# Router logits with the router's weights stationary, and transposed back

## The chip, the cores and the metric

The kernel runs on one core of one Trainium2 chip. The metric is the device time of one execution in microseconds (us); the numbers below are the median of six executions, and one further execution was profiled. All data are 32-bit floats (some indices are 32-bit integers).

## What is computed

Two layers work on 128 graphs of 64 nodes with 256 features, that is 8192 rows (tokens). Each layer is a graph attention inside every graph, followed by a mixture of 8 experts of which each token uses two. Cut to its core:

```python
# layer 0
x = x + gnn(layernorm(x), adj, W, a)          # attention within 64 nodes, elu
x = x + moe(layernorm(x), router_w, w1, b1, w2, b2)
# layer 1
x = x + gnn(layernorm(x), adj, W, a)          # with a leaky slope of 0.2
x = x + moe(layernorm(x), Wg, bg, bias, W1, b1, W2, b2)

def moe(tokens):                               # tokens: (8192, 256)
    logits = tokens @ router_w.T               # (8192, 8): the router
    top2 of the logits, weights by softmax over the two
    for each expert e:                         # hidden 256 (layer 0), 512 (layer 1)
        h = gelu(tokens @ w1[e] + b1[e])       # relu in layer 1
        y = h @ w2[e] + b2[e]
        out += combine[:, e] * y
```

The part in question is the line `logits = tokens @ router_w.T`: for each token 8 sums over 256 features.

## The kernel before

The 8192 rows are taken in blocks of 512 (`TB`), four tiles (`TT`) of 128 partitions (`P`); 16 blocks per layer, 32 in all, numbered by t in the main loop. Three strands of work are interleaved by hand, in an order that the program writes out: on TensorE, VectorE, ScalarE and SyncE, instructions run in the order in which the Python code issues them.

- `attend` (called `a`) is the attention of one block. It is a Python generator: every `yield` ends a stage, and each call `a(n)` issues one more stage. Stages that matter here: the transposes of the normalized block (line 249, tile `pt_g`), the product with the attention's weights (line 288, tile `pw_g`, copied out by ScalarE at line 295), a small VectorE product (line 299, `sm_g`), the scores (lines 307 and 308, `pe_g`), their maximum on VectorE (line 323) and exponential on ScalarE (line 326), the transposes of the attention (line 337, `pp_g`), copied by VectorE and ScalarE (lines 339 and 340), and the product with them (line 346, `po_g`).
- `route` (called `r`) is the router of one block, a generator too: statistics; normalization into `tn` (line 238); transposes of `tn` (line 249, tile `pt_r`), copied to SBUF as `xt_r`, one half by VectorE (line 253) and one by ScalarE (line 255); the router's product into `pl_r` (line 417) and its copy into `lg` (line 426, or 428 and 429 in layer 1), the choice of the best expert; the second best; an exponential; the places in the experts' lists (lines 474 to 492); the writes of the rows to those lists in DRAM by eight indirect DMAs (line 497, on GpSimd's queue); and `plan` (lines 533 to 600), some twenty small VectorE instructions that decide which expert the next slots of 256 rows belong to.
- `Slots` runs the experts on such slots: `x` transposes 256 rows (line 680, copied at line 684), `h` makes the hidden layer (line 749, activation at line 757, which waits for the biases too), `y` the output (line 777, added to its bias at line 785), which indirect DMAs scatter. In layer 1 the output rows are first weighted (line 817). `fetch` lets SyncE load the rows of coming slots (line 609) after it has read the plan's table (line 604), and `ahead` loads the experts' weights.

In the router's product the token tile is the stationary operand (128x128, loaded for every matmul) and the router's weights, 8 columns, are the moving one. The output has tokens on partitions and experts along the free dimension. A 32-bit matmul shows up as two weight loads and two matmul instructions in the profile, a 32-bit transpose as one of each.

The PSUM pool `ps_c` has two buffers for tag "a" (attention) and two for tag "r" (router); the SBUF tag "ex" has three buffers.

Turn t of the main loop (lines 933 to 982) issues stages of the attention of block t+1, of the routing of block t, the last stage of the routing of block t-1 (`r(t - 1)`, the plan), the first two of block t+1 (`r(n)`), and calls of `h`, `x`, `y`. Around the change the order is:

```python
        h(); x(); a(n)       # a(n): the product of line 288
        r(t - 1)             # the plan
        a(n)                 # line 299
        h()
        r(t)                 # transposes of line 249
        slots.fetch()
        if more: x()
        a(n)                 # lines 307 to 326
        r(t)                 # the router's product, lg, first choice
```

Blocks 0 to 2 are worked through before the loop by the list `chains`, in which each turn pops one stage from each chain.

Of the kernel before, what the change touches and what calls it, by code (L numbers as in the profile page):

```python
# [8 lines left out]
F32 = mybir.dt.float32  # L9
# [7 lines left out]
P = 128  # L17
NG = 64
D = 256
KD = D // P  # L20
E = 8
TT = 4
TB = TT * P
# [12 lines left out]
def adj_ffn_kernel(  # L36
# [33 lines left out]
    nc = tc.nc  # L70
# [18 lines left out]
    work = ctx.enter_context(tc.tile_pool(name="work", bufs=3))  # L89
    small = ctx.enter_context(tc.tile_pool(name="small", bufs=2))  # L90
    slot = ctx.enter_context(tc.tile_pool(name="slot", bufs=2))
    ps_c = ctx.enter_context(tc.tile_pool(name="ps_c", bufs=2, space=bass.MemoryType.PSUM))
# [25 lines left out]
    ident = const.tile([P, P], F32, name="ident")  # L118
# [5 lines left out]
    for g in range(2):  # L124
        r = slice(g * NG, (g + 1) * NG)
# [10 lines left out]
    start = const.tile([P, E], F32, name="start")  # L136
# [48 lines left out]
    rw = [const.tile([P, KD, E], F32, name=f"rw{l}") for l in range(2)]  # L185
# [57 lines left out]
    def transposed(src, tag, ptag, name, both):  # L243

        xt = work.tile([P, KD, TB], F32, tag=tag, name=f"xt_{name}", bufs=2)
        for k in range(KD):
            pt = ps_c.tile([P, TB], F32, tag=ptag, name=f"pt_{name}_{k}")
            for t in range(TT):
                nc.tensor.transpose(
                    pt[:, t * P : (t + 1) * P], src[:, t, k * P : (k + 1) * P], ident  # L250
                )
            if k % 2 == 0 and not both:
                nc.vector.tensor_copy(xt[:, k, :], pt)  # L253
            else:
                nc.scalar.copy(xt[:, k, :], pt)
        return xt
# [143 lines left out]
    def route(l, b, blk):  # L400

        name = f"r{l}_{b}"
# [8 lines left out]
        yield  # L411
        tT = transposed(tn, "tT", "r", name, l == 0 and b < FIRST)
        yield
        pl = ps_c.tile([P, TT, E], F32, tag="r", name=f"pl_{name}")
        for t in range(TT):
            for k in range(KD):
                nc.tensor.matmul(  # L417
                    pl[:, t, :],
                    lhsT=tT[:, k, t * P : (t + 1) * P],
                    rhs=rw[l][:, k, :],  # L420
                    start=(k == 0),
                    stop=(k == KD - 1),
                )
        lg = small.tile([P, TT, E], F32, tag="lg", name=f"lg_{name}")
        if l == 0:
            nc.vector.tensor_copy(lg, pl)
# [27 lines left out]
        r = slice(b * TT, (b + 1) * TT)  # L454
# [161 lines left out]
    class Slots:  # L616
# [117 lines left out]
        def h(self):  # L734
            k = self.nh
            self.weighted()
            if k == self.nx or k == self.ny + 2:
                return
            self.nh += 1
            sl = self.all[k]  # L740
            l = sl["l"]
            wc, xT = sl["wc"], sl["xT"]
            hT = slot.tile([P, HC[l], SL], F32, tag="hT", name=f"hT_s{k}")
            for f in range(0, HC[l], 2):
                ph = ps_s.tile([P, 2, SL], F32, tag="ph", name=f"ph_s{k}_{f}", bufs=2)
                for j in range(2):
                    for c in range(KD):
                        o = c * HC[l] * P + (f + j) * P
                        nc.tensor.matmul(  # L749
                            ph[:, j, :],  # L750
                            lhsT=wc[:, o : o + P],
                            rhs=xT[:, c, :],
                            start=(c == 0),
                            stop=(c == KD - 1),
                        )
                for j in range(2):
                    nc.scalar.activation(  # L757
                        hT[:, f + j, :], ph[:, j, :], AF.Gelu if l == 0 else AF.Relu,
                        bias=wc[:, OB1[l] + f + j : OB1[l] + f + j + 1],
                    )  # L760
            sl["hT"] = hT
            if l == 1 and sl["rest"]:
                self.spare(k)

        def y(self):
            k = self.ny
            self.weighted()
            if k == self.nh:
                return
            self.ny += 1  # L770
            sl = self.all[k]
            l = sl["l"]
            wc, hT = sl["wc"], sl["hT"]
            py = ps_s.tile([P, ST, D], F32, tag="py", name=f"py_s{k}")
            for t in range(ST):
                for f in range(HC[l]):
                    nc.tensor.matmul(  # L777
                        py[:, t, :],
                        lhsT=hT[:, f, t * P : (t + 1) * P],
                        rhs=wc[:, O2[l] + f * D : O2[l] + (f + 1) * D],  # L780
                        start=(f == 0),
                        stop=(f == HC[l] - 1),
                    )
            ys = slot.tile([P, ST, D], F32, tag="ys", name=f"ys_s{k}", bufs=4)
            nc.vector.tensor_tensor(  # L785
                ys, py, wc[:, OB2[l] : OB1[l]].unsqueeze(1).to_broadcast([P, ST, D]), ALU.add
            )
            sl["ys"] = ys
            for t in range(ST):
                if l == 0:  # L790
                    ins = nc.gpsimd.indirect_dma_start(  # L791
                        out=res[sl["part"]],
                        out_offset=self.row(sl, t),
                        in_=ys[:, t, :],
                        in_offset=None,
                        bounds_check=2 * N - 1,
                        oob_is_err=False,
                    )
                    unordered(f"res{sl['part']}", ins)
            if l == 1:  # L800
                self.ready = k
            self.ahead()
# [57 lines left out]
    def there(i):  # L860
        return 0 <= i < len(blks) and blks[i]

    def load(i, first=None):
        if there(i):
            k = blks[i]
            if k["l"]:
                assert all(s["l"] or s["part"] != part(k["b"]) for s in slots.all[slots.ny :])
            k["in"] = load_block(k["l"], k["b"], first)
            k["a"] = attend(k["l"], k["b"], k)

    def a(i, n=1):
        if there(i):
            for _ in range(n):
                next(blks[i]["a"], None)

    def r(i, n=1):
        if there(i):
            k = blks[i]
            if "r" not in k:
                k["r"] = route(k["l"], k["b"], k)  # L880
            for _ in range(n):
                next(k["r"], None)
# [15 lines left out]
    place = counted("place", [P, ST], [[P, ST]], 0, 1)  # L898
    att = lambda b: [(a, b)] * 9 + [(a, b, 2), (a, b)]
    chains = [  # L900
        (0, att(0)[3:] + [(r, 0)] * 10),
        (1, att(1)[2:] + [(r, 1)] * 10),
        (2, att(2) + [(r, 2)] * 9),
        (8, att(3) + [(r, 3)] * 2),
        (12, [(a, 4)] * 3),
    ]
# [26 lines left out]
    for t in range(FIRST, len(blks)):  # L933
        n = t + 1
        more = slots.nf - slots.ny > SB or len(slots.all) - slots.ny > SB
        if t + 3 != NB:
            load(t + 3)
        a(n)
        h()
        x()  # L940
        a(n)
        r(t - 1)
        a(n)
        h()
        r(t)
        slots.fetch()
        if more:
            x()
        a(n)
        r(t)  # L950
        if t + 2 != NB:
            a(t + 2)
        y()
        a(n)
        (h if more else x)()
        r(t)
        a(n)
        y()
        a(t + 2, 1 + (t + 2 == NB))
        if more:  # L960
            x()
        a(n)
        r(t)
        h()
        a(n)
        if more:
            y()
        x()
        a(n)
        h()  # L970
        r(n)
        y()
        a(t + 2)
        r(t)
        r(t)
        y()
        slots.fetch()
        x()
        r(n)
        r(t)  # L980
        if t + 3 == NB:
            load(t + 3)
# [57 lines left out]
```

## Time and profile before

| | |
|---|---|
| median of 6 executions | 1726.02 us (1723.2 to 1731.31) |
| profiled execution, its own time | 1729.69 us |
| its span in the profile | 1727.8 us |
| mean granted TensorE clock | 0.888 |
| instructions | 22826 |

How to read the profile: PE is TensorE's matmuls, PEld its weight loads (they overlap PE), DVE is VectorE, ACT ScalarE, POOL GpSimd, SP SyncE; a "q" behind a name is that engine's sequencer or queue. A line of a group or of the order in time names the line of the code, the engine, the operation, the tile written and after the arrow the tiles read, the shape, and how many. In the list of costly groups the numbers behind the bar are busy time in us, mean duration of one in ns, then the engine's idle time just before them and what ended most of it. In the order of time the first two numbers are start and length in us, and in brackets stands the idle time before and what ended it; "remote" there means that the wait ended by an event which fits no end of an instruction at that time. In the list of waits the numbers are the sum in us, how often, and the longest. In the table by stretches, PEclk is the granted TensorE clock as a share of the full one. Each instruction of a row with "x16" is pipelined with the next, so the time to the next row's start says more than the length.

Some more entries of the profile that the prediction uses:

| group | count | mean ns |
|---|---|---|
| line 417, weight load 128x128 for `pl_r` | 512 | 241 (median 192 of a quiet turn) |
| line 249, transposes `pt_r` | 256 | 288 |
| line 255, ScalarE copy 128x512 | 35 | 586 |
| line 253, VectorE copy 128x512 of `pt_r` | 29 | 691 |
| line 340, ScalarE copy 64x256 | 32 | 364 |
| line 295, ScalarE copy 128x258 | 128 | 375 |

### The profile page before, as it was taken

To read this page: it belongs to the slowest core of one execution; us is meant where nothing else is said; L and a number is where in the kernel's file an instruction comes from. 1 tells how busy PE (TensorE), PEld (TensorE's weight loads), DVE (VectorE), ACT (ScalarE), POOL (GpSimd) and SP (SyncE) were. 2 spreads that over 40 slices of the span, in tenths; PEclk is the share of its full clock that TensorE was granted. 3 is DMA by queue.
4 is the path that set the end of the run, shared out by engine and by line. 5 is a ranking of instruction groups with operands and counts; after the bars stand their busy time and mean duration, and the time that the engine had idled before them with its cause. 6 is when DMAs were issued, how large, how long until landed. Compare 5 with 4: busy or idle time off the path is not lost. (4 is left out here: it accounts for less than half of the span.)

```text
span 1727.8 us, 22826 instructions
## 1 busy us (share of the span) xinstructions
PE 1352.0 (78%) x6436; PEld 1141.9 (66%) x6436; DVE 883.0 (51%) x3404; ACT 669.5 (39%) x1567; POOL 766.5 (44%) x742
## 2 busy tenths in 40 slices
PE   6657776767777667666668798888889888889997
PEld 4546655655556546555557677777778777778896
DVE  4555755564454555745555554555556554332332
ACT  4534444444444434333334333333343333223332
POOL 3254544444444454334444355345454444544333
PEclk9668988888888889878889889999999898999999
DMA  6545555575554665656565577577786656688774
GB/s 188 138 144 182 171 159 166 165 213 161 159 177 140 213 201 161 218 165 187 187 208 164 155 224 236 160 202 210 200 229 198 171 142 185 170 232 245 201 205 70
DMA packets 267198, 315.42 MB, mean 183 GB/s; under 512 B 41399, under 2 KB 224318, under 8 KB 267072
## 3 DMA queue, kind: packets, MB, share of 16 engines
q1 hardware_dynamic: 222240, 227.80, 43.5%
q0 software_dynamic: 44832, 86.17, 18.8%
q8 instruction: 51, 0.84, 0.2%
q14 instruction: 75, 0.61, 0.1%
HBM read 215.03 MB, written 102.51 MB: 184 GB/s over the span
## 5 line engine op out<-in xcount | busy, mean ns | idle before, releaser
L749 PE MATMUL ph_s<-xT_s,wc_s 128*128 128x256 f32 x1760 | 430.4, 396 | 64.0 <-DVE xT_s L684 27.9
L777 PE MATMUL py_s<-wc_s,hT_s 128*128 128x256 f32 x1760 | 442.9, 405 | 14.3 <-issue 14.0
L749 PEld LDWEIGHTS ph_s<-xT_s,wc_s 128*128 128x128 f32 x1760 | 343.8, 199 | 132.4 <-DVE xT_s L684 36.4
L777 PEld LDWEIGHTS py_s<-wc_s,hT_s 128*128 128x128 f32 x1760 | 350.3, 204 | 66.6 <-issue 16.6
L820 POOL DMA_INDIRECT out_dram<-ys_s,to_s x142 | 222.9, 1570 | 348.4 <-ACT ys_s L817 244.9
L757 ACT ACTIVATE hT_s<-ph_s,wc_s 128x256 f32<-128x256 f32 x440 | 183.2, 470 | 305.8 <-issue 132.7
L497 POOL DMA_INDIRECT lists<-tn_r,ix_r x256 | 248.7, 972 | 107.5 <-issue 72.4
L791 POOL DMA_INDIRECT res<-ys_s,to_s x156 | 160.1, 1026 | 293.3 <-DVE erc_g L332 179.5
L288 PE MATMUL pw_g<-gw,xt_g 128*128 128x258 f32 x512 | 156.6, 460 | 163.8 <-ACT wh_g L295 134.6
L288 PEld LDWEIGHTS pw_g<-gw,xt_g 128*128 128x128 f32 x512 | 111.1, 229 | 196.2 <-ACT wh_g L295 141.2
L684 DVE COPY xT_s<-px_s 128x512 f32<-128x512 f32 x149 | 102.2, 686 | 234.2 <-remote 151.0
L785 DVE TENSOR_TENSOR ys_s<-py_s,wc_s 128x512 f32<-128x512 f32 x149 | 103.0, 691 | 212.1 <-PE py_s L777 198.9
L817 ACT ACTIVATE ys_s<-ys_s,cf_s 128x256 f32<-128x256 f32 x142 | 64.1, 499 | 148.5 <-DVE ys_s L785 148.3
L417 PE MATMUL pl_r<-rw,xt_r 128*128 128x8 f32 x512 | 81.0, 292 | 47.5 <-DVE xt_r L253 38.5
L417 PEld LDWEIGHTS pl_r<-rw,xt_r 128*128 128x128 f32 x512 | 80.7, 241 | 54.7 <-DVE xt_r L253 42.8
L295 ACT COPY wh_g<-pw_g 128x258 f32<-128x258 f32 x128 | 46.4, 375 | 177.7 <-remote 85.5
L238 ACT ACTIVATE tn_r<-xb_g,nb_r,rs_r 128x256 f32<-128x256 f32 x128 | 66.4, 589 | 81.4 <-DVE nb_r L236 39.2
L238 ACT ACTIVATE xn_g<-xs,nb_g,rs_g 128x256 f32<-128x256 f32 x128 | 66.4, 589 | 64.5 <-DVE nb_g L236 64.5
L680 PE MATMUL px_s<-ident,xg_s 128*128 128x128 f32 x596 | 91.3, 276 | 0.0
L680 PEld LDWEIGHTS px_s<-ident,xg_s 128*128 128x128 f32 x596 | 75.4, 145 | 12.5 <-issue 0.6
L277 POOL TENSOR_SCALAR cap_g<-adj 128x256 f32<-128x256 int32 x32 | 34.6, 1082 | 93.8 <-DMA adj<-in_adj_dram 64.2
L346 PE MATMUL po_g<-wh_g,pT_bd 128*128 128x256 f32 x256 | 69.3, 418 | 7.7 <-ACT pT_bd L340 5.6
(474 smaller groups left out, 1569.7 us busy)
## 6 DMA issues: line engine op xcount, KB each, us to landing
wc_s<-in_w_dram SPq DMA_DIRECT2D x142, 512.0 KB
wc_s<-in_w_dram SPq DMA_DIRECT2D x156, 256.0 KB
xg_s<-lists SPq DMA_DIRECT2D x78, 258.0 KB
xg_s<-lists SPq DMA_DIRECT2D x71, 260.0 KB
yb<-res SPq DMA_DIRECT2D x16, 1024.0 KB
wc_s<-bcat SPq DMA_DIRECT2D x78, 129.0 KB
wc_s<-bcat SPq DMA_DIRECT2D x71, 130.0 KB
xs<-in_x_dram SPq DMA_DIRECT2D x16, 512.0 KB
```

The lines of the kernel that those rows point to most:

```text
L238: nc.scalar.activation(outs(t), xb[:, t, :], AF.Identity, bias=nb[:, t : t + 1], scale=rs[:, t : t + 1])
L288: nc.tensor.matmul(pw, lhsT=xt[:, k, t * P : (t + 1) * P], rhs=gw[l][:, k, :], start=(k == 0), stop=(k == KD - 1),)
L417: nc.tensor.matmul(pl[:, t, :], lhsT=tT[:, k, t * P : (t + 1) * P], rhs=rw[l][:, k, :], start=(k == 0), stop=(k == KD - 1),)
L497: ins = nc.gpsimd.indirect_dma_start(out=lists[l], out_offset=bass.IndirectOffsetOnAxis(ap=ix[:, k, t : t + 1], axis=0), in_=tn[:, t, 0 : ...
L680: nc.tensor.transpose(px[:, c, t * P : (t + 1) * P], xg[:, t, c * P : (c + 1) * P], ident)
L684: nc.vector.tensor_copy(xT, px)
L749: nc.tensor.matmul(ph[:, j, :], lhsT=wc[:, o : o + P], rhs=xT[:, c, :], start=(c == 0), stop=(c == KD - 1),)
L757: nc.scalar.activation(hT[:, f + j, :], ph[:, j, :], AF.Gelu if l == 0 else AF.Relu, bias=wc[:, OB1[l] + f + j : OB1[l] + f + j + 1],)
L777: nc.tensor.matmul(py[:, t, :], lhsT=hT[:, f, t * P : (t + 1) * P], rhs=wc[:, O2[l] + f * D : O2[l] + (f + 1) * D], start=(f == 0), stop=( ...
L785: nc.vector.tensor_tensor(ys, py, wc[:, OB2[l] : OB1[l]].unsqueeze(1).to_broadcast([P, ST, D]), ALU.add)
L791: ins = nc.gpsimd.indirect_dma_start(out=res[sl["part"]], out_offset=self.row(sl, t), in_=ys[:, t, :], in_offset=None, bounds_check=2 * N - 1,
L820: ins = nc.gpsimd.indirect_dma_start(out=out, out_offset=self.row(sl, t), in_=ys[:, t, :], in_offset=None, compute_op=ALU.add,)
```

## The change

The routing gets one more stage. After the transposes, the router's weights (128x8 for each half of the features) become the stationary operand and the transposed tokens (512 columns) the moving one. The product `pq` has 8 partitions (experts) and 512 columns (tokens). ScalarE copies it to SBUF (`lT`), the stage ends, and in the next stage four transposes bring it back into `pl`, 128 partitions by 8 for each of the four tiles. From `lg` on nothing changes.

`pq` takes a turn in the two PSUM buffers of tag "r", `lT` one in the three SBUF buffers of tag "ex".

As there is one stage more, the order gets one more call: `r(t)` in the main loop ahead of `r(t - 1)`, and one more entry in the chains of blocks 0 to 2. In the loop, the routing transposes are thus issued where the plan stood, then come the plan, `a(n)` and `h()`, then `pq` and its copy where the transposes stood, and the transposes back where the router's product stood.

```diff
         tT = transposed(tn, "tT", "r", name, l == 0 and b < FIRST)
         yield
+
+        pq = ps_c.tile([E, TB], F32, tag="r", name=f"pq_{name}")
+        for k in range(KD):
+            nc.tensor.matmul(
+                pq, lhsT=rw[l][:, k, :], rhs=tT[:, k, :], start=(k == 0), stop=(k == KD - 1)
+            )
+        lT = work.tile([E, TB], F32, tag="ex", name=f"lT_{name}")
+        nc.scalar.copy(lT, pq)
+        yield
         pl = ps_c.tile([P, TT, E], F32, tag="r", name=f"pl_{name}")
         for t in range(TT):
-            for k in range(KD):
-                nc.tensor.matmul(
-                    pl[:, t, :],
-                    lhsT=tT[:, k, t * P : (t + 1) * P],
-                    rhs=rw[l][:, k, :],
-                    start=(k == 0),
-                    stop=(k == KD - 1),
-                )
+            nc.tensor.transpose(pl[:, t, :], lT[:, t * P : (t + 1) * P], ident[0:E, 0:E])
         lg = small.tile([P, TT, E], F32, tag="lg", name=f"lg_{name}")
...
-        (0, att(0)[3:] + [(r, 0)] * 10),
-        (1, att(1)[2:] + [(r, 1)] * 10),
-        (2, att(2) + [(r, 2)] * 9),
+        (0, att(0)[3:] + [(r, 0)] * 11),
+        (1, att(1)[2:] + [(r, 1)] * 11),
+        (2, att(2) + [(r, 2)] * 10),
...
         x()
         a(n)
+        r(t)
         r(t - 1)
         a(n)
         h()
```

## The prediction

> **What bounds the kernel now.** I read the engines' busy shares and the costliest groups first, then the busy time by stretch, then TensorE's waits, then two turns of the main loop in order of time. The page first:
>
> ```profile
> PE 1352.0 (78%) x6436; PEld 1141.9 (66%) x6436; DVE 883.0 (51%) x3404; ACT 669.5 (39%) x1567; POOL 766.5 (44%) x742
> L417 PE MATMUL pl_r<-rw,xt_r 128*128 128x8 f32 x512 | 81.0, 292 | 47.5 <-DVE xt_r L253 38.5
> ```
>
> TensorE is the busiest engine, and the router's product (line 417) has 512 instructions, two for each of 8 matmuls in 32 blocks, with 47.5 us of idle time ahead of them. The stretches (turns t=3 to 20, turns 21 to 31, tail):
>
> ```profile
> core 0: us, PE busy (x) PEld busy (x) DVE busy (x) ACT busy (x) POOL busy (x), PEclk, DMA share, GB/s
> 108.00:957.00 849.00, 598.38 (x2852) 495.10 (x2852) 463.54 (x1761) 347.05 (x754) 381.54 (x383) 0.86 0.57 180
> 957.00:1496.00 539.00, 472.16 (x2239) 406.29 (x2239) 291.33 (x1138) 204.97 (x529) 252.54 (x203) 0.92 0.68 191
> 1496.00:1728.00 232.00, 212.26 (x1070) 187.44 (x1070) 71.85 (x272) 66.68 (x155) 91.40 (x62) 0.96 0.72 187
> ```
>
> TensorE is busy 70%, then 88%, then 91%. What it waits for in the first two stretches:
>
> ```profile
> PE pw_g L288 <- ACT wh_g L295: 126.4, 13, 10.0
> ...
> PE pl_r L417 <- DVE xt_r L253: 38.2, 10, 5.1
> ```
>
> In the first stretch one wait of about 10 us in a turn stands ahead of the attention's product (line 288), before the edit's place; the edit doesn't touch it. In the second the wait stands right at the router's product: 38.2 us in 10 turns. A turn of each kind:
>
> ```profile
> 595.57 3.06 PE L749 MATMUL ph_s<-xT_s,wc_s 128*128 128x256 f32 x8
> 598.46 1.04 PE L249 MATMUL pt_r<-ident,tn_r 128*128 128x128 f32 x8
> 599.34 0.60 PE L680 MATMUL px_s<-ident,xg_s 128*128 128x128 f32 x4
> 599.77 0.60 PE L307 MATMUL pe_g<-sm_g,same 128*128 128x256 f32 x2
> 600.21 0.59 PE L308 MATMUL pe_g<-wh_g,ident 128*128 128x256 f32 x2
> 600.64 1.85 PE L417 MATMUL pl_r<-rw,xt_r 128*128 128x8 f32 x16
> ```
>
> ```profile
> 590.08 0.16 DVE L541 SCALAR_TENSOR_TENSOR lf_p<-du_p,at_r 128x8 f32<-128x8 f32 x1
> 593.47 0.17 DVE L594 TENSOR_TENSOR du_p<-du_p,tk_p 128x8 f32<-128x8 f32 x1
> 596.22 0.42 DVE L299 TENSOR_TENSOR sm_g<-imod,wh_g 128x256 f32<-128x256 f32 x1 [2.59 <-ACT wh_g L295]
> 599.10 0.69 DVE L253 COPY xt_r<-pt_r 128x512 f32<-128x512 f32 x1 [2.46 <-PE pt_r L249]
> 602.52 0.19 DVE L426 COPY lg_r<-pl_r 128x32 f32<-128x32 f32 x1 [0.81 <-PE pl_r L417]
> ```
>
> TensorE runs without a gap here; VectorE does the plan (lines 541 to 594, 3.56 us from 590.08 to 593.64) while it would wait anyway. And in the second stretch:
>
> ```profile
> 1235.74 1.04 PE L249 MATMUL pt_r<-ident,tn_r 128*128 128x128 f32 x8
> 1240.59 0.69 DVE L253 COPY xt_r<-pt_r 128x512 f32<-128x512 f32 x1 [6.57 <-remote]
> 1241.33 0.39 PE L417 MATMUL pl_r<-rw,xt_r 128*128 128x8 f32 x2 [3.69 <-DVE xt_r L253]
> 1241.90 2.14 PE L417 MATMUL pl_r<-rw,xt_r 128*128 128x8 f32 x14 [0.17 <-ACT xt_r L255]
> 1250.57 0.69 DVE L785 TENSOR_TENSOR ys_s<-py_s,wc_s 128x512 f32<-128x512 f32 x1 [1.30 <-PE py_s L777]
> ```
>
> TensorE's transposes are recorded as over at 1236.8, yet VectorE's copy of them starts at 1240.59: their end is seen late. I can't name the cause; it comes back in every turn of this stretch.
>
> **TensorE's own sum, per block.** Removed: 16 instructions of line 417. Their next instruction starts 1.70 us after the first (600.64 to 602.34), 106 ns each. Added: 4 instructions of 512 columns. A 256-column one of line 749 takes 3.45/16 = 216 ns in the chain of waits; by columns 431 ns, so 4 x 431 = 1.73 us. From below, if width cost nothing, 4 x 216 = 0.86. I take 1.73, since the 128-column transposes (0.43 for 4, 109 ns) already show time going with columns. Then 4 transposes with 8 moving columns: at most the 0.43 of four 128-column ones (line 680); at least 0.22, since a transpose's weight load is recorded 51 ns shorter than a product's (139 against 190 ns) and 106 - 51 = 55 ns. I take 0.33. Net 1.73 + 0.33 - 1.70 = +0.36 us, ends -0.62 and +0.46. So the edit doesn't save TensorE time; it splits one product into two dependent pieces with ScalarE between.
>
> [...]
>
> **The added copy.** ScalarE moves 8x512 from PSUM: line 255's 128x512 copy takes 586 ns, and 64 partitions cost no less than 128 (364 against 375 ns), so 0.59; lower end the 128x2 copy's 0.16. Behind it on ScalarE stands the attention's exponential, which waits for later TensorE work; the weighted-output and hidden-layer activations come before it. The added PSUM tile (tag "r", two buffers) and SBUF tile (tag "ex", three) take buffers whose last readers are data it needs anyway or are long done: nothing, and 0.6 us a turn (one copy) if not.
>
> **What moves.** The extra r(t) puts the routing transposes ahead of the plan and of h(). No DMA is issued by that step. On TensorE 0.88 us goes ahead of 2.89 us; on VectorE the copy of line 253 now stands ahead of the plan's 3.56 us and waits for its transposes. SP waits for the plan: its list loads come some 6 us later, at 600.5 instead of 595.0; its next issue waits until 605.17 now, so this hides; without that cover it costs what it passes 605.
>
> First kind of turn, from 595.57: transposes to 596.45, ph 599.34, product 601.07, px 601.50, pe 602.37, transposes back 602.70, against 602.34. VectorE: copy 596.05 to 596.74, plan to 600.30, line 299 to 600.72, 0.78 us before pe needs it. Then the maximum of line 323 ends at 603.33 instead of 601.72, because pe is now behind the product. ScalarE's exponentials (1.34), residual (2.06), table load (1.28), hidden layer (0.84) and half copy (0.36) follow from 603.4 and end at 609.3 instead of 608.63: the product of line 346 moves by +0.66. That I take for 12 turns: 7.9 us. In the last 6 turns of the stretch the attention's transposes (line 337) already wait for VectorE (19.0 us in 7 waits), so they get VectorE's delay, 0.8 at line 426 and 1.6 at line 323; I take 1.3: 7.8. Together +16, ends -11 (18 x -0.62) and +29 (18 x 1.6).
>
> Second kind: the product fills 1.73 us of the wait. If its end is seen at 1240.5 as the present late ends are, ScalarE does the hidden layer to 1241.37, the copy to 1241.96, and the transposes back end near 1242.5 instead of 1243.89: -1.4. The chain behind has slack on VectorE of 0.59 (before line 428) and 1.30 (line 785), so no more than -1.9 can be gained. The copy of line 253 may be seen late, which takes part away; I take -1.0, ten times: -10, ends -19 and +23 (third case below).
>
> The granted clock: it is 0.51 from 1243 to 1250 and 1.00 before and after. A shorter wait may keep it up, but TensorE would then wait for VectorE's chain, so the -1.9 holds still.
>
> [...] In this trace gaps of 2.94 us were followed by half clock in some turns (763 us) and not in others (814.8).
>
> Before the loop three blocks pass through at 51, 71 and 88 us, with gaps around them; copy and transposes add 0.59 + 0.43 each if serial, 3 us, or nothing. I take +2.
>
> Sum: 16 - 10 + 2 = +8 us on the profiled execution's 1729.69 (span 1727.8 and 1.9 around it), 1737.7. That execution lies 3.7 above the median of 1726.02, so for the median: 1734.
>
> **The rivals.** *The second stretch wins.* The wait of 38.2 us speaks for it, VectorE's slack limits it: -19 there, and the first stretch pays only TensorE's +0.36 x 18 = 6.5: 1726 - 12.5 = 1713. *Nothing measurable.* Gain and loss cancel: 1726. *The plan gets stuck.* In the second stretch the transposes' end is seen late by 3.5 us or more in its new place too. The copy at 1240.6 would then hold the plan (to 1244.8), line 299 (1245.3), pe (1246.2), and through VectorE's 3.75 us of line 265 line 337 by +2.3: ten times +23, so 16 + 23 + 2 = +41, 1767. It decides from a copy start later than about 1237. Against it: ScalarE's copies of line 295 are seen on time up to 1232.5, and the transposes would end at 1232.7 and 1233.2. That the edit doesn't do what it says I count to the first rival: a product of 0.86 would take 0.87 off each of 32 blocks, 28 us, at most 1706.
>
> **How the numbers follow.** Forecast 0.49 (1724 to 1746, mostly above 1729.5), first rival 0.27, nothing measurable 0.12, stuck plan 0.12. About 0.2%, 3.5 us, is what a measurement can tell from none. Faster 0.27, same 0.13 (with a little of the forecast), slower 0.60. The range leaves out the far ends of both rivals: 1710 to 1758; the forecast's own is 1724 to 1746.
>
> **What would show it.** Right: four 512-column instructions 430 ns apart; line 253's VectorE copy before line 541 in every turn; line 323 later by about 1.6 us after the long wait in the first stretch; a wait of 2 to 3 us before the transposes back in the second. Wrong: a product nearer 0.9 us, a long wait of the first stretch that changes from 10 us, or line 253 starting after 1237 in a turn of the second (the same place counted from its line 288).

## The result, and the profile after

The changed kernel takes 1731.79 us (median of 23 executions) against 1724.83 us for the kernel before (49 executions on the same chip). The ratio is 1.0036, with a 95% interval from 1.0025 to 1.0048: slower by 7 us. The profiled execution has a span of 1735.7 us against 1727.8. From the product on, line numbers are 2 to 4 higher than before; after the routing they are 2 higher.

The page of the changed kernel, and its groups kept apart by shape (busy time in us, mean ns of one, then the idle time ahead of them and what ended it):

```profile
PE 1351.2 (78%) x6180; PEld 1076.7 (62%) x6180; DVE 878.1 (51%) x3404; ACT 686.6 (40%) x1599; POOL 766.9 (44%) x742
```

```profile
L417 PE MATMUL pq_r<-xt_r,rw 128*8 128x512 f32 x128 | 65.2, 630 | 9.3 <-ACT xt_r L255 5.0 <-DVE xt_r L253 4.3
...
L421 ACT COPY lT_r<-pq_r 8x512 f32<-8x512 f32 x32 | 18.2, 569 | 23.9 <-PE pq_r L417 23.9
L425 PE MATMUL pl_r<-ident,lT_r 8*128 8x8 f32 x128 | 14.6, 219 | 27.9 <-ACT lT_r L421 27.9
```

TensorE has 256 instructions fewer and is as busy as before (1352.0). The idle time ahead of the product fell from 47.5 to 9.3 us, and 27.9 us now stand ahead of the transposes back. The stretches of the same turns:

```profile
108.00:982.00 874.00, 614.99 (x2708) 470.95 (x2708) 461.47 (x1772) 357.23 (x770) 380.10 (x383) 0.87 0.55 173
982.00:1504.00 522.00, 459.06 (x2160) 375.50 (x2160) 290.68 (x1141) 209.73 (x539) 255.47 (x205) 0.96 0.72 199
1504.00:1736.00 232.00, 210.52 (x1060) 185.45 (x1060) 72.00 (x272) 68.13 (x159) 91.40 (x62) 0.96 0.71 188
```

The first stretch got longer (849 to 874 us) and the second shorter (539 to 522 us), with a granted clock of 0.96 there instead of 0.92. The start of each block's product of line 474 (`pn_r`, 476 after) marks the end of its turn; differences between such starts, summed over turns, tell where the time went:

| turns | before, us | after, us | difference |
|---|---|---|---|
| start to block 2 | 96.5 | 96.5 | 0.0 |
| 3 | 43.7 | 47.1 | +3.4 |
| 4 to 8 | 199.9 | 199.6 | -0.3 |
| 9 | 42.5 | 50.7 | +8.2 |
| 10 to 14 | 244.7 | 245.7 | +1.0 |
| 15 to 20 | 310.8 | 327.4 | +16.6 |
| 21 to 31 | 582.4 | 561.0 | -21.5 |
| tail | 207.3 | 207.6 | +0.3 |

So the small result is a loss of some 29 us (turns 3 and 9 to 20) and a gain of some 21 us (turns 21 to 31). Turn 14, the one that the prediction worked through, in order of time after the change:

```profile
605.03 3.81 PE L288 MATMUL pw_g<-gw,xt_g 128*128 128x258 f32 x8 [9.96 <-ACT wh_g L295]
...
611.66 1.88 PE L417 MATMUL pq_r<-xt_r,rw 128*8 128x512 f32 x4
613.48 0.66 PE L682 MATMUL px_s<-ident,xg_s 128*128 128x128 f32 x4
...
615.35 0.41 PE L425 MATMUL pl_r<-ident,lT_r 8*128 8x8 f32 x4
615.69 1.99 PE L779 MATMUL py_s<-wc_s,hT_s 128*128 128x256 f32 x8
615.91 0.42 DVE L323 TENSOR_REDUCE emx_g<-ee_g 128x4 f32<-128x256 f32 x1
...
621.94 0.36 ACT L340 COPY pT_bd<-pp_g 64x256 f32<-64x256 f32 x1
```

From start to start the product takes 1.82 us (611.66 to 613.48) and the four transposes back 0.34 us (615.35 to 615.69). Counted from line 288, the maximum of line 323 comes 1.55 us later than before and the half copy of line 340 0.61 us later (16.91 against 16.30). A turn of the second stretch:

```profile
1253.37 1.03 PE L249 MATMUL pt_r<-ident,tn_r 128*128 128x128 f32 x8
1254.00 0.69 DVE L253 COPY xt_r<-pt_r 128x512 f32<-128x512 f32 x1 [2.77 <-PE pw_g L288]
...
1257.79 1.88 PE L417 MATMUL pq_r<-xt_r,rw 128*8 128x512 f32 x4
...
1260.24 0.84 ACT L759 ACTIVATE hT_s<-ph_s,wc_s 128x256 f32<-128x256 f32 x2 [5.16 <-PE pq_r L417]
...
1262.46 0.56 ACT L421 COPY lT_r<-pq_r 8x512 f32<-8x512 f32 x1
1263.07 0.41 PE L425 MATMUL pl_r<-ident,lT_r 8*128 8x8 f32 x4 [2.34 <-ACT lT_r L421]
```

VectorE's copy starts 0.63 us after the transposes do, so here their end is seen on time. It is 0.63 to 0.64 us in each of turns 22 to 30, where the kernel before has 4.8 to 5.3. The late-seen end is now that of the next TensorE work: ScalarE's half of the hidden layer (line 759) waits 5.16 us, and through the copy of line 421 TensorE waits 2.34 us instead of some 3.7.

### The profile page after: what moved, and what is told of

It reads as the page before. It is cut to its first block, busy times and chain, and to the rows that moved or that the text cites. A ratio compares the mean times of both kernels' runs of the same rounds, so it can differ in the third digit from the quotient of the medians.

```text
span 1735.7 us, 22335 instructions
## 1 busy us (share of the span) xinstructions
PE 1351.2 (78%) x6180; PEld 1076.7 (62%) x6180; DVE 878.1 (51%) x3404; ACT 686.6 (40%) x1599; POOL 766.9 (44%) x742
## 3 DMA queue, kind: packets, MB, share of 16 engines
q1 hardware_dynamic: 222240, 227.80, 43.5%
## 5 line engine op out<-in xcount | busy, mean ns | idle before, releaser
L751 PE MATMUL ph_s<-xT_s,wc_s 128*128 128x256 f32 x1760 | 419.3, 388 | 62.0 <-DVE xT_s L686 27.9
L751 PEld LDWEIGHTS ph_s<-xT_s,wc_s 128*128 128x128 f32 x1760 | 332.4, 193 | 123.8 <-DVE xT_s L686 36.4
L779 PEld LDWEIGHTS py_s<-wc_s,hT_s 128*128 128x128 f32 x1760 | 345.8, 202 | 66.0 <-issue 16.6
L253 DVE COPY xt_r<-pt_r 128x512 f32<-128x512 f32 x29 | 20.0, 691 | 151.5 <-PE pt_r L249 110.7
L346 PE MATMUL po_g<-wh_g,pT_bd 128*128 128x256 f32 x256 | 65.7, 401 | 9.5 <-ACT pT_bd L340 8.1
L417 PE MATMUL pq_r<-xt_r,rw 128*8 128x512 f32 x128 | 65.2, 630 | 9.3 <-ACT xt_r L255 5.0
```

Of the source, the lines that this page charges most:

```text
L346: nc.tensor.matmul(po[h][:, j, :], lhsT=pT[:, 2 * h + j, :], rhs=wh[:, 2 * h + j, 0:D], start=True, stop=True,)
L751: nc.tensor.matmul(ph[:, j, :], lhsT=wc[:, o : o + P], rhs=xT[:, c, :], start=(c == 0), stop=(c == KD - 1),)
L779: nc.tensor.matmul(py[:, t, :], lhsT=hT[:, f, t * P : (t + 1) * P], rhs=wc[:, O2[l] + f * D : O2[l] + (f + 1) * D], start=(f == 0), stop=( ...
```

## Experiments

Theory: in the second stretch the gain comes from transposes issued earlier, not from the wide product; everywhere the loss comes from the attention's scores (lines 307, 308), now behind the product, so that VectorE's chain to line 337 starts later. Rivals: TensorE's added time is the loss; the wide product is the gain; the plan, pushed back on VectorE, is the loss.

The runs went to three chips, one for each group, and the kernel before takes 1707.21 us on the first of these chips, 1454.72 on the second, 1453.51 on the third. Which chip gave the result above is not recorded; I count it as a fourth, since its executions of the kernel before (1716.01 to 1733.15 us) all lie above those of the first group (1694.20 to 1713.79). "The first chip" below is that of the result. Ratios and sums are compared inside a group, or between the second and third group, which agree. Each edit is shown against the changed kernel or against the kernel before, as is said with it.

### First group: parts of the change (the kernel before: 1707.21 us)

**The plan first.** In the loop of the changed kernel the two calls change places:

```diff
-        r(t)
         r(t - 1)
+        r(t)
         a(n)
```

> The changed kernel with one swap: in each turn the plan (r(t - 1)) again comes before the routing transposes (r(t)), so that VectorE does the plan during the long wait and the copy of the transposed tokens behind it. Theory (the loss of turns 9 and 16, +8.2 and +5.1 us, and part of turns 18 and 19 is the plan standing behind that copy): those turns lose no more than 1 to 2 us each, the last eleven keep their gain of about 22 us, time about 1716 to 1721, ratio to before 0.995 to 0.998. Rival (the loss is TensorE's own +0.4 us a turn and the exponentials behind the product): no more than 3 us better than the changed kernel, ratio 1.002 to 1.004.

Ratio 1.0057 [1.0031, 1.0083]. The expected 0.995 to 0.998 was missed; the rival's 1.002 to 1.004 lies at the lower end of the interval.

**The new order with the old product** (the plan behind the transposes, as in the change), against the kernel before:

```diff
         tT = transposed(tn, "tT", "r", name, l == 0 and b < FIRST)
         yield
+        yield
         pl = ps_c.tile([P, TT, E], F32, tag="r", name=f"pl_{name}")
...
+        r(t)
         r(t - 1)
```

> The moved transposes alone: the extra stage and call stay, but the product is the old one with the tokens stationary, issued where it was. Theory (the order makes both the loss and the gain, the product's form only some tenths): turns 9 and 16 still lose about 8 and 5 us, the wait before the router's product in the last eleven turns is gone, their gain is at least 15 us; time within 8 us of the changed kernel, more likely below it since the maximum no longer waits for the product. Rival (the product in two pieces makes the gain by filling the wait): the last eleven turns gain less than 8 us and the time is above 1735.

Ratio 1.0141 [1.0101, 1.0182]. The expectation compares with the changed kernel, which was not run on this chip, so that part stays undecided.

**The new product in the old order:** transposes, product and copy stand together where the transposes stood; against the changed kernel:

```diff
-        r(t)
         r(t - 1)
         a(n)
         h()
         r(t)
+        r(t)
```

> The new product alone: transposes, product and copy are issued together where the transposes stood before, behind the plan and h(). Theory: the product waits for the copies of the transposed tokens (about 0.5 us in the first stretch, the whole late end of some 4 us in the second) and the gain of the last eleven turns is gone or turned into a loss; the first stretch loses 0.4 to 1.2 us a turn, but nothing special in turns 9 and 16; time 1735 to 1755. Rival (the product's form makes the gain): below 1722.

Ratio 1.0347 [1.0308, 1.0385], a larger loss than expected.

**The change from turn 21 on only,** against the changed kernel (the old product in the other branch is left out here):

```diff
-        pq = ps_c.tile([E, TB], F32, tag="r", name=f"pq_{name}")
+        turned = NB * l + b >= 21
+        if turned:
+            pq = ps_c.tile([E, TB], F32, tag="r", name=f"pq_{name}")
...
-        r(t)
+        if t >= 21:
+            r(t)
         r(t - 1)
         a(n)
         h()
-        r(t)
+        r(t, 1 if t >= 21 else 2)
```

> The change only from turn 21 on; before that the order and the product of the kernel before. Theory (the turns add up: turn 3 to 20 lose, turn 21 to 31 gain about 22 us by the two traces): 1701 to 1708, ratio 0.986 to 0.990. Rival (the gain of the last turns only makes up for what the earlier ones left behind, such as other transfers in flight): less than 8 us faster than before, ratio above 0.995.

Ratio 0.9911 [0.9886, 0.9937]: on this chip faster than the kernel before, at the edge of what was expected. The sums by turns, all four on one chip:

| turns | plan first | order only | product only | from turn 21 |
|---|---|---|---|---|
| 3 to 8 | 243.1 | 252.0 | 243.0 | 238.7 |
| 9 | 42.2 | 49.8 | 43.0 | 40.6 |
| 10 to 14 | 244.6 | 254.5 | 243.9 | 240.2 |
| 15 to 20 | 318.8 | 318.8 | 322.4 | 302.0 |
| 21 to 31 | 559.5 | 554.9 | 603.0 | 559.1 |

The last column has the order of the kernel before up to turn 20. Turns 21 to 31: with the product, moving the transposes takes 603.0 to 559.5, 43.5 us; with the transposes moved, ahead of the plan in both, the new product costs 559.1 - 554.9 = 4.2 us. The gain is the move's. Where the product stays behind its transposes, the old wait is there as before (TensorE's waits, product only, second stretch; sum, times, longest in us):

```profile
PE pq_r L417 <- DVE xt_r L253: 45.4, 11, 4.9
```

The plan was a loss where nothing covers it. With the order alone, TensorE's waits in the first stretch:

```profile
PE pe_g L307 <- DVE sm_g L299: 36.6, 13, 6.2
```

The small VectorE product of line 299 stands behind the plan, and the scores wait for it. In the changed kernel TensorE works on the 1.82 us of the product meanwhile, except in the two turns that make two plans, a regular one and a closing one (turn 9, `du_p_8r`, and turn 16). Elsewhere its waits there are at most 0.6 us. The changed kernel's turn 9 on the first chip:

```profile
367.66 0.15 DVE L543 SCALAR_TENSOR_TENSOR lf_p<-du_p,at_r 128x8 f32<-128x8 f32 x1
...
374.60 0.16 DVE L596 TENSOR_TENSOR du_p_8r<-du_p,ns_p_8r 128x8 f32<-128x8 f32 x1
374.87 0.42 DVE L299 TENSOR_TENSOR sm_g<-imod,wh_g 128x256 f32<-128x256 f32 x1
375.34 1.22 PE L307 MATMUL pe_g<-sm_g,same 128*128 128x256 f32 x2 [4.31 <-DVE sm_g L299]
```

Two plans hold VectorE for 7.1 us, TensorE waits 4.31 us, and line 307's two instructions then take 1.22 instead of 0.60 us. With the plan first, turn 9 takes 42.2 us, 1.5 more than with the old order on the same chip; in the changed kernel on the first chip it lost 8.2. The first run's expectation was missed all the same: turns 15 to 20 still take 318.8 us against 302.0 in the old order. That loss is not the plan's: turns 17 and 18 make no plan, and lose 1.4 and 4.7 us on the first chip. Turn 16 too still takes 52.1 us against 48.0: its wait at line 307 is gone, but line 337 waits 4.19 us instead of 2.98.

### Second group: before and after where nothing is seen late (the kernel before: 1454.72 us)

The two kernels themselves, unedited:

> The kernel before, unchanged, for a trace on the same chip as the next three: its turns are the base for theirs. All theories: the same order of waits as in the first trace of it (long wait at line 288 up to turn 20, wait at line 417 from turn 21 on); its time may differ from chip to chip by some 1%.

> The changed kernel, unchanged, on the same chip. All theories: ratio 1.002 to 1.006. By turns against the trace of before on this chip: turn 9 about +8, turns 15 to 20 together about +16, turns 21 to 31 together about -21.

The kernel before gives 1453.55 us. The changed one gives 1518.92, ratio 1.0446 [1.0424, 1.0469]. Both expectations were missed by far. TensorE's waits of the kernel before in turns 21 to 31 on this chip:

```profile
PE pp_g L337 <- DVE ee_g L333: 17.1, 7, 2.8
...
PE pl_r L417 <- DVE xt_r L253: 0.3, 1, 0.3
```

The wait of 38.2 us ahead of the router's product is 0.3 us here, and the 10 us ahead of line 288 are missing too, apart from one wait at the start of the loop. So there is nothing to gain, and the price of the change stands alone. I call such a chip quiet.

**Two mixtures:** the change from turn 21 on (product and order) with the plan first, and the new order with the plan first and the old product in all turns. The first one's loop, and then the second one's, against the kernel before:

```diff
         r(t - 1)
+        if t >= 21:
+            r(t)
         a(n)
         h()
-        r(t)
+        r(t, 1 if t >= 21 else 2)
```

```diff
         r(t - 1)
+        r(t)
         a(n)
```

> Old order and old product up to turn 20; from turn 21 on the new product, and the transposes moved ahead but behind the plan (plan first). Theory (as with the change in the late turns alone, 0.9911; the plan has room there): ratio 0.988 to 0.993, no difference to it that can be told. Rival (plan first frees VectorE so that the maximum and the choice come earlier): below 0.988.

> In all turns: plan first, then the transposes, moved ahead of h(), with the old product at its old place. Theory (with the plan out of the way, moving the transposes costs nothing in the first stretch, and it is the new product that delays the exponentials and the first choice there; the wait at the router's product goes away in the second): first stretch within 5 us of before, turns 21 to 31 at least -15, ratio 0.988 to 0.994. Rival (the new product is needed for the gain): turns 21 to 31 gain less than 8 us, ratio above 0.996.

The first gives 1484.32 us, ratio 1.0198 [1.0171, 1.0225]; the second 1460.81, ratio 1.0043 [1.0020, 1.0065]. Both were expected below 1, with the gain that this chip doesn't have. Turns 21 to 31 take 504.7 us before, 530.5 after, 532.7 in the first mixture and 504.3 in the second: the moved transposes cost nothing there, the new product in its place costs 26 us.

### Third group: what the product's price is made of (the kernel before: 1453.51 us)

The changed kernel again, as the base:

> The changed kernel itself, as the base for the three other runs on the same chip. Two chips have given 1.0036 and 1.0446 for it. Theory A (the price of the change is that the scores of lines 307 and 308 stand behind the product, so VectorE's chain and with it line 337 come later; the gain is the wait ahead of the router's product that goes, and only some chips have that wait): about 1.00 if the run of the kernel before is near 1710 to 1725 us, about 1.045 if it is near 1455 us. Rival B (the price is TensorE's own added time, 0.36 us in each of 32 blocks): 1.007 on both.

1520.52 us, ratio 1.0451 [1.0434, 1.0468], as by theory A. TensorE's added time at 0.36 us a block would be 12 us; measured are 67. One turn, before (turn 28, second group's chip) and after (turn 27, this chip), in order of time:

```profile
1092.20 0.60 PE L307 MATMUL pe_g<-sm_g,same 128*128 128x256 f32 x2
...
1094.59 0.42 DVE L323 TENSOR_REDUCE emx_g<-ee_g 128x4 f32<-128x256 f32 x1
...
1101.50 0.60 PE L337 MATMUL pp_g<-ident,ee_g 128*64 128x128 f32 x4 [2.59 <-DVE ee_g L333]
1101.94 3.62 PE L777 MATMUL py_s<-wc_s,hT_s 128*128 128x256 f32 x16
```

```profile
1102.16 1.88 PE L417 MATMUL pq_r<-xt_r,rw 128*8 128x512 f32 x4
1103.97 0.70 PE L307 MATMUL pe_g<-sm_g,same 128*128 128x256 f32 x2
...
1106.54 0.42 DVE L323 TENSOR_REDUCE emx_g<-ee_g 128x4 f32<-128x256 f32 x1
...
1113.36 1.03 PE L337 MATMUL pp_g<-ident,ee_g 128*64 128x128 f32 x4 [3.83 <-DVE ee_g L333]
1114.18 4.61 PE L779 MATMUL py_s<-wc_s,hT_s 128*128 128x256 f32 x16
```

From the maximum of line 323 to line 337 it is 6.9 us before (1094.59 to 1101.50) and 6.8 after: VectorE's chain (line 265, line 785 or 787, line 333) sets line 337. Scores behind the product start that chain later, the wait grows from 2.6 to 3.8 us, and what follows it runs slower (1.03 and 4.61 us for 0.60 and 3.62).

**The earlier transposes alone, from turn 21 on, with the old product,** against the kernel before:

```diff
         tT = transposed(tn, "tT", "r", name, l == 0 and b < FIRST)
         yield
+        yield
...
         r(t - 1)
+        if t >= 21:
+            r(t)
         a(n)
         h()
-        r(t)
+        r(t, 1 if t >= 21 else 2)
```

> The old product; only from turn 21 on are the routing transposes issued earlier, behind the plan. Turns 3 to 20 are those of the kernel before. Theory A: on a chip with the wait of 38 us ahead of the router's product, turns 21 to 31 lose that wait and get 20 us or more shorter, ratio 0.985 to 0.990; on a chip without it 0.998 to 1.002. Rival (the gain in turns 21 to 31 comes from the wide product, not from the earlier transposes): 1.000 on both.

1461.18 us, ratio 1.0050 [1.0035, 1.0065], a little more than expected. Turns 21 to 31 take 504.4 us against 504.7. Nearly all of the excess lies before turn 4: block 3's product of line 474 starts at 143.8 us instead of 137.3, and the span is 1458.8 instead of 1451.6. The longer chains of blocks 0 to 2 (one stage more for each, as in the change) are the one edit that acts there.

**The scores first:** product and copy stay, but the scores and their maximum go ahead of them, and line 265's work ahead of the transposes back. The plan stands first. Against the changed kernel, cut:

```diff
         sm = small.tile([P, TT], F32, tag="esm", name=f"esm_{name}")
+        if between:
+            between.pop()()
...
+        r(t - 1)
         r(t)
-        r(t - 1)
         a(n)
         h()
-        r(t)
         slots.fetch()
+        between.append(lambda: r(t))
+        a(n)
...
+        if t + 2 != NB:
+            a(t + 2)
         if more:
             x()
-        a(n)
         r(t)
-        if t + 2 != NB:
-            a(t + 2)
         y()
```

> The wide product and its copy by ScalarE stay, but the scores of lines 307 and 308 and their maximum on VectorE are issued ahead of it, and the exponentials, the weighted sum of the next attention block and the expert's transposes ahead of the transposes back; the plan stands first. Theory A: VectorE's chain starts as early as in the kernel before, so the wait at line 337 goes back from 3.8 us to about 2.7 us a turn in turns 21 to 31 and no half clock follows it; on a chip without the long wait 1.000 to 1.012 (at most 32 x 0.36 us of TensorE's time is left), on a chip with it 10 us or more below the changed kernel. Rival B: within 0.3% of the changed kernel.

1470.61 us, ratio 1.0110 [1.0093, 1.0127], 50 us below the changed kernel on the same chip, where the rival expects at most 0.3%. The same place in its order of time:

```profile
1064.38 1.88 PE L421 MATMUL pq_r<-xt_r,rw 128*8 128x512 f32 x4
...
1066.92 0.41 PE L429 MATMUL pl_r<-ident,lT_r 8*128 8x8 f32 x4 [0.67 <-ACT lT_r L425]
...
1072.83 0.60 PE L341 MATMUL pp_g<-ident,ee_g 128*64 128x128 f32 x4 [1.41 <-DVE ee_g L337]
1073.27 3.62 PE L783 MATMUL py_s<-wc_s,hT_s 128*128 128x256 f32 x16
```

The wait is 1.41 us and the expert's product runs at its 3.62 us again. Turns 21 to 31 take 507.6 us and turns 15 to 20 233.6, against 504.7 and 233.8 before and 531.9 and 254.4 after. The run moves more than one call, so it doesn't tell the scores' place from that of line 265; both start VectorE's chain earlier. In turns 21 to 31 the plan put first is not the cause, since the first mixture has it too and takes 532.7 us.

What is left, 17 us, lies nearly all in turns 3 to 14, which take 426.2 us against 409.0 before and 430.6 after. So the scores' place does not explain the loss there. Turn 3 has 3.9 us of it with the longer chains alone (44.2 for 40.4 in the run before this one). Most of the rest comes with the new product: turns 4 to 8 and 10 to 14 take 152.8 and 178.7 us in the second mixture, with the old product, and 159.8 and 183.9 here. TensorE's added 0.46 us a turn would be 4.6 of these 12 us; no run singles out the remainder.

**A longer wait and nothing else:** the kernel before with two more VectorE instructions, whose result nobody reads, behind line 265, for turns 14 to 29.

```diff
+            idle = work.tile([P, 320], F32, tag="idle", name=f"idle_{name}", bufs=1)
+            for k in range(2):
+                nc.vector.scalar_tensor_tensor(
+                    idle,
...
+                )
         yield
         stats = ln_stats(xs, name)
```

> The kernel before with two more VectorE instructions of 128x320 (about 0.57 us each by line 265's 0.47 us for 256 columns) behind line 265 in turns 14 to 29, whose result nobody reads: the wait of line 337 gets about 1.1 us longer, as in the changed kernel, with no wide product anywhere. Theory A2 (a wait that passes some 3 us costs the clock as well): on a chip without the long waits the waits at line 337 in turns 21 to 29 go from 2.7 to about 3.8 us, a stretch of lower clock follows each, and turns 21 to 31 get 2.4 to 3.0 us longer each, 22 to 27 us in all, ratio 1.018 to 1.025. Rival (the wait costs its length alone): 1.1 us a turn, 10 us in turns 21 to 31, ratio 1.008 to 1.012. On a chip with the long waits line 337 waits less, and it costs 0 to 1.1 us a turn by both.

1482.11 us, ratio 1.0196 [1.0182, 1.0209].

```profile
1079.90 0.60 PE L347 MATMUL pp_g<-ident,ee_g 128*64 128x128 f32 x4 [3.76 <-DVE ee_g L343]
1080.34 5.30 PE L787 MATMUL py_s<-wc_s,hT_s 128*128 128x256 f32 x16
```

The two instructions take 0.557 us each. Turns 24, 25, 27 and 28 got 2.7, 2.6, 2.7 and 2.9 us longer: 1.1 for the wait, 1.7 for the expert's product at a lower clock (5.30 for 3.62 us, with a mean clock of 0.76 against 1.00 over the 7 us from the end of line 337's wait). Turns 26 and 29 got 1.0 longer: in turn 26 the kernel before has the lower clock too (0.76 after a wait of 2.73 us), and in turn 29 the clock stayed full here (1.00 after 3.58 us). The total came out as expected, its place only in part: turns 21 to 31 lost 15.4 us instead of 22 to 27, also since turns 21 to 23 lost 0.8 each; turns 15 to 20 lost 11.5.

## Why the prediction was right

**The total:** forecast +8 us, measured +7 on the first chip. The forecast case came in, 1734 against 1731.79 us. But two of its parts were off by some 10 us, with opposite signs: turns 4 to 20 lost 25.6 us (forecast 16), turns 21 to 31 gained 21.5 (forecast 10). That they cancelled is luck.

**TensorE's own sum and the copy were right.** Product 1.82 us (forecast 1.73), transposes back 0.34 (0.33), so net +0.46 (0.36, upper end 0.46); ScalarE's copy 0.57 (0.59).

**First stretch, "+0.66 for 12 turns: 7.9 us".** The working was right in the turn that it was made for: line 323 1.55 us later (forecast 1.6), the half copy of line 340 0.61 us later, the long wait still 9.96 us. But turns 4 to 8 and 10 to 14 changed by 0.7 us together. The delay does not reach the end of the turn. In turn 14 the next hidden layer waits for its input and starts 23.93 us after line 288 instead of 23.61, so half of the delay is left; the expert's product behind it then takes 2.22 us instead of 3.21, and the turn ends earlier than before. For the other turns I have not singled it out.

**First stretch, "plan to 600.30, line 299 0.78 us before pe needs it".** This holds for one plan, barely: VectorE's copy starts 0.97 us after the transposes instead of the 0.48 assumed, line 299 ends at 614.24 and the scores start at 614.28. Turns 9 and 16 make two plans, and cost 8.2 and 5.1 us. The step failed by taking one turn for all; the plan put first shows it in turn 9. In turn 16 the same wait stands at line 307 (3.67 us), but with the plan first the turn still lost 4.1 us, at line 337, so that its loss is the plan's is not shown.

**First stretch, "last 6 turns, 1.3 each: 7.8 us".** Without turn 16 the other five lost 11.5 us. The mechanism is right: line 337 waits for VectorE, before 19.0 us in 7 waits and now, in the first stretch,

```profile
PE pp_g L337 <- DVE l_r L445: 24.7, 7, 4.2
```

The size was too small. The granted clock was left out of this part: over the 7 us from the end of line 337's wait it is 0.61 to 0.76 in the five turns with waits of 3.96 to 4.19 us, while in the kernel before, with waits of 2.74 to 2.97 us, it is 1.00 in three turns of six and 0.57 to 0.79 in the others. The kernel before with a longer wait shows that part by itself (0.76 after 3.76 us in turn 27), but on a quiet chip.

**Second stretch, "-1.0, ten times; max -1.9".** Measured -21.5 us in 11 turns, 2.0 each, and 3.9 in turns 22 and 23, beyond the limit. The reason why it could gain was right: the product fills the wait, and transposes issued earlier are seen on time (line 253 at 1254.00, with a wait of 2.0 to 2.7 us ahead of the transposes back in turns 22 to 30, as foreseen). "The -1.9 holds still" was wrong: it counted VectorE's slack at an unchanged clock, while the granted clock of the stretch went from 0.92 to 0.96, and that of turns 22 and 23 from 0.91 and 0.94 to 1.00. At 0.92, 459 us of busy TensorE would be 459 x 0.96 / 0.92 = 479, an upper estimate of 20 us for what the clock can be worth.

**Before the loop, "+2".** +3.4 us, and they appear in turn 3; and 1.5 to 6.5 us up to there in the runs on quiet chips that have the longer chains (1.3 in one that has not).

**SP's list loads, "this hides".** Right: counted from line 288 in turn 14, the load of line 609 is issued 9.0 us after it instead of 3.0, and the next issue, that of line 651, 13.5 instead of 13.2.

**The rivals.** "The plan gets stuck" with its condition (a copy later than 1237) did not occur, since the transposes' end is seen on time in the new place; but the plan is stuck for another reason where the product doesn't cover it (order only: 36.6 us). "The second stretch wins" was right in the second stretch and failed on the first: it charged that one 6.5 us, and it lost 25.6 behind turn 3. "Nothing measurable" is excluded by the interval.

**What no part of the prediction had:** that the 38 us wait is seen on some chips only. Where it is absent the same change costs 4.5%: the gain is missing, and turns 3 to 20 lose 38 to 42 us instead of 29.

## What to carry to other kernels

When two products change places on one engine, follow the slower engine's chain behind the one that now comes second: here the change cost 67 us on a quiet chip where TensorE's own added time is 32 x 0.46 = 15 us, and 50 of the 67 went when the scores stood ahead of the 1.8 us product again, so that VectorE's chain started earlier: in turns 24 to 29 line 337 then waited 1.3 to 1.4 us instead of 3.8, and the expert's product behind it took 3.62 us instead of 4.6 to 6.1. Work out every kind of turn (the one with two plans too), and test the parts of a change apart: here the earlier transposes were the gain, and the product that it came with was the loss. A gain that fills a wait which the profile can't name should be measured on a second chip.

## What the runs showed of the hardware

**The clock after a wait.** On the quiet chips, in turns 21 to 31, waits of line 337 from 2.54 to 2.76 us were followed by full clock over the next 7 us in 10 of 12 cases (kernel before, and early transposes with the old product). Waits of 3.58 to 3.83 us were followed by a mean clock of 0.59 to 0.80 in 11 of 12 (changed kernel, and longer wait). The window of one such wait, from its end on (TensorE's clock is the third number from the end):

```profile
1079.90:1086.90 7.00, 7.00 (x27) 5.88 (x28) 3.64 (x17) 1.63 (x4) 2.79 (x2) 0.76 0.69 183
```

So on the quiet chips these two groups of waits differ in the clock that followed, with exceptions on both sides. On the first chip waits shorter than those of the second group were followed by a lower clock too: waits of 2.32 to 2.69 us ahead of the transposes back by a mean clock of 0.53 to 0.76 in 6 of 8 cases, and waits of 2.97 us at line 337 in the kernel before by 0.57 twice and 1.00 three times. The length of the wait alone therefore does not tell the clock here, and it is best read from the trace of the chip in question.

**Chips differ by up to 19%.** The kernel before takes 1725, 1707, 1455 and 1454 us in the four groups of runs (1724.83 / 1453.51 = 1.19). In the two slower ones TensorE's ends are seen late by other engines in certain places, on the first chip as waits of 3.3 to 5.1 us at the router's product and of 7.2 to 10.0 at line 288, with a mean clock of 0.50 to 0.78 over the next 7 us; in the others these waits are missing. Each chip was visited once, so chip and time of the visit are not told apart. No run here shows the cause, and it stays open.

**What stays open besides.** The scores' place was tested on a quiet chip alone; that it is also the loss of turns 15 to 20 on the first chip is argued from the same wait at line 337. No version was faster than the kernel before on both kinds of chip. The change from turn 21 on is 0.9% faster on the chip of 1707 us and, with the plan first, 2.0% slower on a quiet one. By the sums, the early transposes with the old product from turn 21 on and unlengthened chains should gain on the former (554.9 against 559.1 us in turns 21 to 31 is 4 us more than that version) and cost nothing on the latter; this was not tried on a chip with the long waits.
